# A two-network graph kernel: the second network's first pieces in batches of three slices, some of it on GpSimd, and one column less in two of three multiplications

## The chip, the cores and the metric

One core of a Trainium2 chip runs the whole program. The metric is device time in microseconds (us) of one execution; a kernel's time is the median of its runs. Four engines compute: TensorE (PE in the profile, with its weight loads as PEld), VectorE (DVE), ScalarE (ACT) and GpSimd (POOL). SP issues most transfers, POOL the indirect ones.

## The reference, cut to what matters

Two graph networks run one after the other on the same 100,000 edges and 6,250 nodes of 128 features, each with a residual sum and a layer norm around it:

```python
x = _layernorm(x + _L0_gnn_ref(x, edge_index, edge_type_8, ...), axis=-1)   # relational, three layers
x = _layernorm(x + _L1_gnn_ref(x, edge_index, W_in, b_in, W_out, b_out), axis=-1)
```

The change touches the second network alone:

```python
h = x @ W_in + b_in                                   # 64 columns
deg = jax.ops.segment_sum(ones, row, num_segments=N)
edge_weight = deg_inv_sqrt[row] * deg_inv_sqrt[col]
acc = h
cur = h
for _ in range(3):
    cur = jax.ops.segment_sum(cur[col] * edge_weight[:, None], row, num_segments=N)
    acc = acc + cur
return (acc / 4) @ W_out + b_out
```

So three multiplications by the same sparse matrix A (how often each pair of nodes is joined), with a scaling by `deg_inv_sqrt` before and after each.

## The kernel before, in words

The 6,250 nodes are 49 blocks (`NBLK`) of 128. Nine **slices** (`NSL`) hold every ninth block: slices 0 to 3 have six blocks, slices 4 to 8 five (`FLD` is 6).

**The first network** fills nine tenths of the time: indirect loads on POOL (L1080) bring the rows of `h_d`, PE sums them by one-hot matrices (L1083), DVE adds the sums into `agg` (L1688). Beside it the kernel counts edges into a dense matrix of packed counts in DRAM, `a_d`, two four-bit counts in each byte and four bytes in a 32-bit word.

**The second network** begins when `agg` is whole, in three steps.

1. **Node rows** (L1796 to L1809). In groups of four blocks, PE transposes each block of `agg` into the PSUM tile `pt` (L1801; five buffers, `ps_w`) and multiplies it by `w_mid` into `ph` (L1803; two buffers, `ps_s`). DVE takes mean and variance of each block from `pt` (L1806, L1807, into `mv`). ACT copies `pt` to `x_nm` (L1808) and `ph` to `acc` (L1809). Then, for all 49 blocks at once, `ve` is made (L1810) and `rsqrt` (L769 to L774: one square root on ACT, five small DVE operations) gives `rs`.
2. **First pieces** (L1827 to L1834). For each slice DVE scales `acc` by `rs` (L1830), adds the bias (L1831), scales by `dis` into `z` (L1833), and `split` writes `z` as three bf16 parts that add up to it: ACT copy (L1821), DVE difference (L1822), ACT copy (L1823), DVE difference (L1824). The parts stand in `three[0]`, 192 columns for each block, and a 193rd column (`C3` is 3 * 64 + 1) holds ones.
3. **Three multiplications** (L1881 to L1925, `k` from 0 to 2). For each of nine output slices `sl` and each of nine input slices `c0`: a load of `packed` from `a_d` (L1891), two DVE operations that take out the four-bit counts as 8-bit floats into `u` (L1893, L1894; three buffers), and 30 or 36 matmuls, one for each input block and output block (L1899), into three PSUM tiles `po` out of the same five buffers that `pt` uses. There are 49 * 49 = 2401 matmuls for each `k`. After an output slice, DVE adds the three parts (L1914 to L1916), copies the sum of the ones column (L1918, only for `k == 0`: it is compared with the degrees), scales and adds to `acc`, and splits again for the next `k`. With `k == 1` the first norm of `x_nm` (`first_norm`, L1837 and L1839) is written between the matmuls; with `k == 2` the output head (L1851 to L1877).

**Order.** These parts are written with a tile framework that places all waits and makes each engine's queue itself: instructions are not bound to the order of the source, and a later line can go ahead where the earlier ones have to wait for data or for a buffer. Each engine then runs its queue strictly in order. (Only the first network pins some of its instructions.)

Of the kernel before, what the change touches and what calls it, by code (L numbers as in the profile page):

```python
# [8 lines left out]
F32 = mybir.dt.float32  # L9
# [8 lines left out]
P = 128  # L18
# [501 lines left out]
def sorted_path(  # L520
# [79 lines left out]
    FILL = 16  # L600
    KP = R // 2
# [16 lines left out]
    assert HT % GT == 0 and HC * GPB <= 512 and SUB * R == P and T1 % P1 == 0  # L618
# [1174 lines left out]
    mv = late.tile([P, NBLK, 2], F32, name="mv")  # L1793
    ve = late.tile([P, NBLK], F32, name="ve")
    rs = late.tile([P, NBLK], F32, name="rs")
    for c in range(0, NBLK, 4):  # L1796
        n = min(4, NBLK - c)
        pt = ps_w.tile([P, 512], F32, name="pw")
        ph = ps_s.tile([P, 4, H], F32, name="ps")
        for j in range(n):  # L1800
            nc.tensor.transpose(pt[:, j * P : (j + 1) * P], agg[:, (c + j) * P : (c + j + 1) * P], ident)  # L1801
        for j in range(n):
            nc.tensor.matmul(ph[:, j, :], agg[:, (c + j) * P : (c + j + 1) * P], w_mid, start=True, stop=True)  # L1803
        for j in range(n):
            st = op.tile([P, 6], F32, name="st_r")
            nc.vector.bn_stats(st, pt[:, j * P : (j + 1) * P])  # L1806
            nc.vector.bn_aggr(mv[:, c + j, :], st)  # L1807
        nc.scalar.copy(x_nm[:, c : c + n, :], pt[:, : n * P].rearrange("p (b f) -> p b f", f=P))  # L1808
        nc.scalar.copy(acc[:, c : c + n, :], ph[:, :n, :])  # L1809
    nc.vector.tensor_scalar_add(ve, mv[:, :, 1], EPS)  # L1810
    rsqrt(late, rs, ve, [P, NBLK], "ln1")

    def scale_of(d, sl):
        part = d[:, sl::NSL]
        n = part.shape[1]
        return part[:, :, None].to_broadcast([P, n, H]), n

    def split(to, z, sl):
# [5 lines left out]
        nc.vector.tensor_tensor(t[:, :, 2 * H : 3 * H], z, t[:, :, H : 2 * H], op=OP.subtract)  # L1824


    for sl in range(NSL):  # L1827
        part = acc[:, sl::NSL, :]
        sc_, n = scale_of(rs, sl)
        nc.vector.tensor_tensor(part, part, sc_, op=OP.mult)  # L1830
        nc.vector.tensor_tensor(part, part, b_in_r[:, None, :].to_broadcast([P, n, H]), op=OP.add)  # L1831
        z = tp.tile([P, FLD, H], F32, name="z")
        nc.vector.tensor_tensor(z[:, :n, :], part, scale_of(dis, sl)[0], op=OP.mult)  # L1833
        split(three[0], z[:, :n, :], sl)  # L1834
# [46 lines left out]
    for k in range(3):  # L1881
        cur, nxt = three[k % 2], three[(k + 1) % 2]
        for sl in range(NSL):
            fields = range(0, len(range(sl, NBLK, NSL)))
            po = [ps_w.tile([P, 512], F32, name="pw") for _ in range(FLD // 2)]
            out_of = lambda f: po[f // 2][:, (f % 2) * C3 : (f % 2 + 1) * C3]
            for c0 in range(NSL):
# [9 lines left out]
                for d, b in enumerate(blocks):  # L1897
                    for f in fields:
                        nc.tensor.matmul(out_of(f), bytes_[f % 2][:, d, :, f // 2], cur[:, b, :],  # L1899
# [84 lines left out]
```

## Time and profile before

| | us |
|---|---|
| median of 3 runs (3521.61 to 3531.9) | 3530.43 |
| the profiled execution | 3529.98 |
| its span, first to last instruction | 3528.1 |
| first network and counting, until the last `agg` sum | 0 to 2832.1 |
| node rows (L1801 first) | from 2832.2 |
| first matmul of L1899 | 2867.1 |
| second multiplication begins | 3076.1 |
| third multiplication begins | 3277.1 |
| last matmul of L1899 | 3509.1 |

The profile is one execution. Times in it are microseconds from the start of the span. In a timeline row stand: start, duration, engine, line, operation, written and read tiles, form, count, and in brackets how long the engine had been idle before and what released it. "x2" is two instructions merged into one row. In rows by stretch stand: the stretch, its length, and for each engine the busy time and number of instructions, then PEclk (the clock granted to PE, as a share of the full one), the share of DMA time and GB/s.

### The profile page before, as it was taken

The page shows a single profiled execution, that of the slowest core. Times are in us where ns is not written, and L with a number is a line of the kernel's source. Part 1 is how long each engine was busy: PE and PEld are TensorE (multiplying, and loading weights), DVE is VectorE, ACT ScalarE, POOL GpSimd, SP SyncE. Part 2 cuts the span into 40 slices and gives each one's busy share as a digit, 9 for nine tenths or more (in the row PEclk, how much of TensorE's full clock was granted, in tenths as well). Part 3 has the DMA queues.
Part 4 walks back from the last instruction along what each step waited for, and adds up shares of the span by engine and source line. Part 5 has one row for each costly group of instructions (what it writes and reads, how often), then busy time and mean ns, then how long its engine had stood idle before and what let it go on. Part 6 is the DMA issues. An engine that isn't in the chain of part 4 may idle for free.

```text
span 3528.1 us, 54660 instructions
## 1 busy us (share of the span) xinstructions
PE 2695.5 (76%) x17110; PEld 2161.4 (61%) x17110; DVE 2125.9 (60%) x6259; ACT 916.4 (26%) x2360; POOL 2083.9 (59%) x2083
## 2 busy tenths in 40 slices
PE   5866667776689666677775986666677579999998
PEld 3454447554646555555554565555555479999997
DVE  7766558644644666666475266666643476646566
ACT  3400007521565655555143510000000020000000
POOL 5777777777757777777774767777777700000000
PEclk9955565576588555555855975555567579999999
DMA  6612222232275222222423842222232234545452
GB/s 203 234 54 63 70 56 59 59 94 71 60 249 189 65 69 67 68 72 68 102 72 90 323 127 75 76 76 78 78 94 71 64 103 138 157 133 158 130 141 77
DMA packets 422817, 373.31 MB, mean 106 GB/s; under 512 B 89934, under 2 KB 370286, under 8 KB 422516
## 3 DMA queue, kind: packets, MB, share of 16 engines
q1 hardware_dynamic: 347832, 230.32, 21.3%
q0 software_dynamic: 66240, 135.79, 13.7%
q10 hardware_dynamic: 8444, 3.61, 0.4%
q8 instruction: 136, 2.23, 0.2%
q14 instruction: 165, 1.35, 0.1%
HBM read 250.74 MB, written 178.62 MB: 122 GB/s over the span
## 4 chain that ended last, share of the span: by engine, by line
PE 41%; DMA 37%; DVE 10%; issue 6%; POOL 5%; ACT 0%; DVEq 0%; POOLq 0%; ACTq 0%
DMA gt<-h_d,gidx 36%; PE pw L1899 16%; PE pw L979 7%; PE ps L1083 7%; POOL gt L1080 5%; PE pw L1384 2%; PE pw L1630 2%; DVE row L1616 1%; PE pw L1411 1%; PE pw L992 1%; DVE had L1589 1%; DVE agg L1688 1%; PE ps L1857 1%; PE pw L1558 0%; DVE dst_hot L1612 0%
## 5 line engine op out<-in xcount | busy, mean ns | idle before, releaser
L1080 POOL DMA_INDIRECT gt<-h_d,gidx x1770 | 1768.9, 999 | 546.8 <-DMA gt<-h_d,gidx 235.6
L1083 PE MATMUL ps<-o,gt 128*128 128x48 f32 (+1 forms) x4140 | 1136.3, 389 | 638.1 <-DMA gt<-h_d,gidx 562.1
L1083 PEld LDWEIGHTS ps<-o,gt 128*128 128x128 f32 x4140 | 936.5, 289 | 928.8 <-DMA gt<-h_d,gidx 752.3
L1616 DVE TENSOR_SCALAR row<-iota_c,e_tab,e_tab 128x252 bf16<-128x252 int16 x1232 | 425.7, 352 | 361.0 <-PE pw L1630 357.5
L1899 PE MATMUL pw<-three,u 128*128 128x193 bf16 x7203 | 616.4, 248 | 15.0 <-issue 9.9
L1899 PEld LDWEIGHTS <-u 128*128 128x128 fp8e3 x7203 | 602.9, 98 | 22.6 <-issue 10.0
L1442 ACT ACTIVATE near<-iota_b,e_tab 128x128 bf16<-128x128 bf16 x782 | 304.7, 391 | 747.7 <-PE pd L1455 443.6
L1630 PE MATMUL pw<-dst_hot,row 128*126 128x128 bf16 x2464 | 447.5, 320 | 54.1 <-DVE row L1616 49.5
L1630 PEld LDWEIGHTS <-row 128*126 128x126 bf16 x2464 | 353.9, 224 | 66.8 <-DVE row L1616 57.2
L1589 DVE SCALAR_TENSOR_TENSOR had<-had,keep,pw 126x256 int32<-126x256 int32 x616 | 292.8, 475 | 11.9 <-PE pw L1630 10.9
L979 PE MATMUL pw<-w,xT 128*128 128x512 f32 x588 | 282.2, 613 | 0.0
L1080 POOL DMA_INDIRECT gt<-x_d,xidx x200 | 191.5, 958 | 136.3 <-PE pw L1630 33.2
L1688 DVE TENSOR_TENSOR agg<-agg,ps 128x48 f32 x885 | 179.0, 202 | 142.5 <-PE ps L1083 107.3
L1443 ACT ACTIVATE near<-iota_b,e_tab 128x49 bf16<-128x49 bf16 x782 | 250.5, 321 | 0.0
L1893 DVE TENSOR_SCALAR u<-packed 128x640 int32<-128x640 int32 (+1 forms) x243 | 126.9, 522 | 203.0 <-PE pw L1899 200.6
L1612 DVE TENSOR_TENSOR dst_hot<-iota_f,e_tab 128x512 bf16<-128x512 f32 x308 | 211.6, 687 | 0.1
L980 ACT COPY hs<-pw 128x512 f32<-128x512 f32 x294 | 171.2, 586 | 121.4 <-PE pw L979 115.5
L1358 ACT CAST x<-xc 128x512 bf16<-128x512 f32 x21 | 13.0, 621 | 673.5 <-PE pw L1384 541.5
L1446 ACT ACTIVATE near<-near,ones 128x708 bf16<-128x708 bf16 x196 | 172.9, 882 | 5.7
L1384 PE MATMUL pw<-x,u 128*128 128x385 bf16 x735 | 172.0, 375 | 0.0
L1111 DVE TENSOR_TENSOR z<-z,ps 128x56 f32 x300 | 63.3, 211 | 179.5 <-PE ps L1083 164.2
L979 PEld LDWEIGHTS pw<-w,xT 128*128 128x128 f32 x588 | 105.2, 194 | 89.7 <-issue 84.1
(400 smaller groups left out, 2174.2 us busy)
## 6 DMA issues: line engine op xcount, KB each, us to landing
a_d<-had SPq DMA_DIRECT2D x616, 126.0 KB
h_d<-hs SPq DMA_DIRECT2D x147, 512.0 KB
packed<-a_d SPq DMA_DIRECT2D x135, 320.0 KB
packed<-a_d SPq DMA_DIRECT2D x108, 384.0 KB
gt<-h_d,gidx POOLq DMA_INDIRECT x1770
c_d<-had SPq DMA_DIRECT2D x62, 196.0 KB
packed<-c_d SPq DMA_DIRECT2D x21, 448.0 KB
x_d<-xc SPq DMA_DIRECT2D x24, 256.0 KB
```

What stands on the lines that cost most here:

```text
L979: nc.tensor.matmul(ph, xT[:, b * P : (b + 1) * P], w[:, c : c + 512], start=True, stop=True)
L1080: nc.gpsimd.indirect_dma_start(out=gt, out_offset=None, in_=table[:, :], in_offset=bass.IndirectOffsetOnAxis(ap=at[:, t : t + 1], axis=0))
L1083: pin(nc.tensor.matmul(pa, gt, o, start=first_, stop=last))
L1384: nc.tensor.matmul(sums[d][:, :C3D], us[d % 2][:, i, :, d // 2], x3[:, i, :], start=(c == 0 and i == 0), stop=(c * CH + i == NBLK - 1))
L1442: nc.scalar.activation(near[:, j, :P], iota_b, AF.Abs, bias=src_lo[:, k : k + 1], scale=-1.0)
L1443: nc.scalar.activation(near[:, j, P:], iota_b[:, :NBLK], AF.Abs, bias=src_blk[:, k : k + 1], scale=-1.0)
L1589: pin(nc.vector.scalar_tensor_tensor(now[:HB, : 2 * P], had[:HB, : 2 * P], keep[:HB, s : s + 1], p[:HB, : 2 * P], op0=OP.mult, op1=OP.add))
L1612: pin(nc.vector.tensor_tensor(hots[i // TS], iota_f[:, None, :].to_broadcast([P, TS, P]), flat(e_lo)[:, i : i + TS, None].to_broadcast([P, ...
L1616: pin(nc.vector.tensor_scalar(rows[i][:, : 2 * HB], iota_c[:, : 2 * HB], e_col[:, s, j : j + 1], e_val[:, s, j : j + 1], op0=OP.is_equal, ...
L1630: pin(nc.tensor.matmul(sums[s][:HB, c * P : (c + 1) * P], row[:, c * HB : (c + 1) * HB], hots[u // TS][:, u % TS, :], start=(j == 0 and c ...
L1688: pin(nc.vector.tensor_add(to, to, pa))
L1899: nc.tensor.matmul(out_of(f), bytes_[f % 2][:, d, :, f // 2], cur[:, b, :], start=(b == 0 and f % 2 == 0), stop=(c0 == NSL - 1 and d == m ...
```

## The change: what it does

- Node rows are made by slices, not by consecutive blocks: `node_rows` takes three blocks (or the two that are left of five) of a slice, so there are 18 groups in place of 13. The work on each block is the same. ACT copies `acc` before `x_nm`.
- They come in three batches of three slices (`SLB`): the blocks of slices 0 to 2 (18 blocks), `ve` and `rsqrt` for these alone, their first pieces; then slices 3 to 5 (16 blocks), then 6 to 8 (15 blocks). `mv`, `ve` and `rs` get 54 columns, so that a batch is a regular part of them; a POOL memset fills the five that no block has.
- In the second and third batch two of the five DVE operations of the first pieces go to POOL: the bias (L1831) and the last difference (L1824), 12 instructions.
- L1899 reads and writes 193 columns for `k == 0` alone, 192 for `k` of 1 and 2.

```diff
+    SLB = 3
...
-    for c in range(0, NBLK, 4):
-        n = min(4, NBLK - c)
+    mv = late.tile([P, FLD * NSL, 2], F32, name="mv")
+    nc.gpsimd.memset(mv[:, NBLK:, :], 1.0)
...
+    def node_rows(blocks):
+
+        n, at = len(blocks), slice(blocks[0], blocks[-1] + 1, NSL)
         pt = ps_w.tile([P, 512], F32, name="pw")
         ph = ps_s.tile([P, 4, H], F32, name="ps")
...
+        nc.scalar.copy(acc[:, at, :], ph[:, :n, :])
+        nc.scalar.copy(x_nm[:, at, :], pt[:, : n * P].rearrange("p (b f) -> p b f", f=P))
...
-    def split(to, z, sl):
+    def split(to, z, sl, third=nc.vector):
...
-        nc.vector.tensor_tensor(t[:, :, 2 * H : 3 * H], z, t[:, :, H : 2 * H], op=OP.subtract)
-    for sl in range(NSL):
+        third.tensor_tensor(t[:, :, 2 * H : 3 * H], z, t[:, :, H : 2 * H], op=OP.subtract)
+    def first_parts(sl, third):
...
         nc.vector.tensor_tensor(part, part, sc_, op=OP.mult)
-        nc.vector.tensor_tensor(part, part, b_in_r[:, None, :].to_broadcast([P, n, H]), op=OP.add)
+        third.tensor_tensor(part, part, b_in_r[:, None, :].to_broadcast([P, n, H]), op=OP.add)
...
+        split(three[0], z[:, :n, :], sl, third)
+
+    for s0 in range(0, NSL, SLB):
+        for sl in range(s0, s0 + SLB):
+            blocks = list(range(sl, NBLK, NSL))
+            for i in range(0, len(blocks), FLD // 2):
+                node_rows(blocks[i : i + FLD // 2])
+        var = by_slices(mv[:, :, 1], s0)
+        nc.vector.tensor_scalar_add(by_slices(ve, s0), var, EPS)
+        rsqrt(late, by_slices(rs, s0), by_slices(ve, s0), [P, FLD, SLB], f"ln1_{s0}")
+        for sl in range(s0, s0 + SLB):
+            first_parts(sl, nc.gpsimd if s0 else nc.vector)
...
-            out_of = lambda f: po[f // 2][:, (f % 2) * C3 : (f % 2 + 1) * C3]
+            cols = C3 if k == 0 else C3 - 1
+            out_of = lambda f: po[f // 2][:, (f % 2) * C3 : (f % 2) * C3 + cols]
...
-                        nc.tensor.matmul(out_of(f), bytes_[f % 2][:, d, :, f // 2], cur[:, b, :],
+                        nc.tensor.matmul(out_of(f), bytes_[f % 2][:, d, :, f // 2], cur[:, b, :cols],
```

## The prediction

> **What bounds the kernel now.** I read the chain of waits on the page first: over the whole span it is the gathers of the first network, which the change leaves alone.
>
> ```profile
> DMA gt<-h_d,gidx 36%; PE pw L1899 16%; PE pw L979 7%; PE ps L1083 7%; POOL gt L1080 5%; PE pw L1384 2%; PE pw L1630 2%; DVE row L1616 1%; PE pw L1411 1%; PE pw L992 1%; DVE had L1589 1%; DVE agg L1688 1%; PE ps L1857 1%; PE pw L1558 0%; DVE dst_hot L1612 0%
> ```
>
> So what counts is L1899's 16% and the short stretch before it. Second, the busy times by stretch from the last sum of `agg` (2832.1) on; the last row is a steady slice of the second multiplication.
>
> ```profile
> 2832.20:2850.50 18.30, 18.27 (x90) 18.30 (x91) 8.12 (x55) 5.02 (x12) 0.00 (x0) 0.50 0.64 191
> 2850.50:2857.20 6.70, 6.54 (x61) 6.24 (x60) 6.17 (x43) 3.64 (x11) 0.00 (x0) 1.00 0.00 0
> 2857.20:2867.10 9.90, 0.00 (x0) 0.03 (x1) 9.35 (x27) 4.07 (x10) 0.00 (x0) 0.68 0.42 119
> 2867.10:2878.10 11.00, 11.00 (x108) 10.52 (x108) 11.00 (x27) 4.55 (x10) 0.00 (x0) 0.83 0.01 3
> 2878.10:2881.00 2.90, 0.04 (x2) 0.01 (x1) 2.90 (x8) 1.37 (x4) 0.00 (x0) 1.00 0.00 0
> ...
> 3100.90:3125.40 24.50, 24.50 (x296) 24.50 (x294) 12.75 (x33) 1.04 (x2) 0.00 (x0) 1.00 0.47 132
> ```
>
> The columns are PE, PEld, DVE, ACT, POOL, then PE's clock. PE bounds the first 18.3 us at half clock (DVE is busy 8.12 of them), PE and DVE together the next 6.7. Then DVE alone bounds 9.9 us in which PE has nothing, and again 2.9 us. A steady slice has PE full and DVE half empty. Third, the chain and the timeline give the paces:
>
> ```profile
> 2838.22 1.60 PE ps L1803 x8
> 2840.68 1.60 PE ps L1803 x8
> ...
> 3079.86 226.13 PE pw L1899 x2703
> ```
> ```profile
> 2861.75 1.03 DVE L1830 TENSOR_TENSOR acc<-acc,rs 128x384 f32<-128x384 f32 x2
> 2862.70 1.02 DVE L1831 TENSOR_TENSOR acc<-acc,b_in_r 128x384 f32<-128x384 f32 x2
> ...
> 2867.10 11.03 PE L1899 MATMUL pw<-three,u 128*128 128x193 bf16 x108 [9.94 <-issue]
> ...
> 2880.37 0.57 DVE L1893 TENSOR_SCALAR u<-packed 128x768 int32<-128x768 int32 x1
> ```
>
> Groups of four blocks start 2.46 us apart at half clock: 0.614 us a block. L1899 takes 226.13 / 2703 = 83.66 ns a matmul at full clock, 24.6 us for a six-block slice. A six-block DVE operation of the first pieces takes (2862.70 - 2861.75) / 2 = 0.47 us, a five-block one 0.405 (the same two rows at 2875: 0.81 for two). L1899 starts when slice 0's parts are written (2867.0). After 108 matmuls, which are the first three input slices, PE stands still because the fourth `u` (2880.37) stood in DVE's queue behind the first pieces of later slices.
>
> Slice 0 of the first multiplication took 2867.1 to 2898.3, 31.2 us against 24.6 steady: 2.9 of standing still and 3.7 of half clock (3.8 us at its start, 3.4 after the stop, at half rate). Slice 1 lost 1.6 waiting for DVE to empty PSUM.
>
> **The change, part by part.** *Node rows.* 49 blocks as before; 18 groups cost PE nothing extra, since the pace is the sum over blocks. PE finishes 18 blocks at 2832.2 + 18 x 0.614 = 2843.3, about when DVE has their statistics (0.26 us a block, L1806 start to start); so DVE is idle 6 us instead of some 10. That is where the batches gain.
>
> *DVE's work before the first matmul.* The queues are not in source order (L1837, written for `k == 1`, runs from 2883.7 to 2922.5, in the first multiplication), but earlier lines go first where they are ready: no `u` was made until the statistics were at their end (2857.2), though PE could have used none sooner. The matmuls also need three of the five PSUM buffers that the transposes of all 49 blocks are waiting for. So I expect L1899 behind nearly all node rows, and its first `u` behind nearly all statistics. From 2843.3: `rsqrt` 1.2 (six operations of about 0.2 around 2860), first pieces of three slices 15 x 0.47 = 7.05, 31 more blocks of statistics 31 x 0.263 = 8.15, second `rsqrt` 1.2, the two opening DVE operations of slices 3 to 5, 6 x 0.43 = 2.6, the third `rsqrt` 1.2, the first `u` 0.93 (two operations, 0.47 each): 22.3, so 2865.6. Between 2864.4 (third `rsqrt` later) and this plus what POOL costs.
>
> *POOL's share.* It takes 12 DVE operations away, about 5 us of DVE, but the bias addition stands between two DVE operations of its slice, and behind L1833 waiting in DVE's queue stand the statistics and `u`, which PE waits for. No POOL arithmetic on two tensors is in the trace. Its nearest rows:
>
> ```profile
> L1155 POOL IOTA iota_s<- 128x616 f32 x1 | 0.7, 668 | 0.0
> L1782 POOL MEMSET three<- 128x49 bf16 x2 | 0.5, 384 | 3.1 <-PE ps L1083 3.1
> ...
> masks.py:199 POOL TENSOR_SCALAR_AFFINE_SELECT ident<-ident 128x128 f32<-128x128 f32 x1 | 0.3, 282 | 0.0
> ```
>
> With 0.10 us fixed (the one-element memset), the iota's rate gives 0.46 us for 384 elements, the selection, which reads one tensor, 0.65, the strided memset 2.3. I take 0.9: above the selection, since two tensors are read. Six of the twelve fall before the first matmul. Whether DVE can run beside them no row shows; between nothing and 6 x 0.9 = 5.4 I take half, 2.7: start at 2868.3, **1.2 later** than 2867.1. The ends are 2864.4 (2.7 earlier) and, at 2.3 with DVE held throughout, 2865.6 + 13.8 = 2879.4 (12.3 later).
>
> The Trainium skill speaks against this part: "SBUF — State Buffer", section "Who interferes with whom", says that a DVE operation with two SBUF inputs and a GpSimd operation that reads SBUF exclude each other for a whole instruction. "GPSIMD Engine Reference", section 3.1, gives some 2.6 cycles an element at 1.2 GHz for two inputs, an estimate of 0.83 us for 384. By these the start would be 2865.6 + 6 x 0.83 = 2870.6 and the time 3526.4.
>
> *Slice 0.* At the start only slices 6 to 8 are left to DVE: 9 operations (3.7 us) and eight `u` (7 us), plus POOL's, against 24.6 us of matmuls. So the 2.9 stop goes, and the second stretch of half clock with it; the first stays, as PE is half idle before. 31.2 becomes 24.6 + 1.9 = 26.5: **4.7 less**, between 1.8 (the stop stays) and 6.6. What hides the `u` is DVE's spare half; if that is gone, the stop of 2.9 is the price.
>
> *Slice 1.* Its stop comes from first norms queued before the emptying of PSUM, and these remain, only earlier. Between 0 and 1.6 I take **0.8 less**. The third `rsqrt`, five more ACT copies a side and the memset run beside DVE's queue and PE: nothing; uncovered, under 2 us.
>
> *The column.* 4802 matmuls lose one. The rate by columns: at full clock twelve matmuls of 385 columns start within 1.97 us,
>
> ```profile
> 2639.95 0.99 PE L1384 MATMUL pw<-x,u 128*128 128x385 bf16 x5
> ...
> 2641.92 0.98 PE L1384 MATMUL pw<-x,u 128*128 128x385 bf16 x5
> ```
>
> 164 ns each, so (164 - 83.66) / 192 = 0.418 ns a column: **2.0 less**. Beyond its columns (193 x 0.418 = 80.7) a matmul costs 3.0 ns; both forms have an odd count, and an even one may save part of that. The 128-column matmuls of L1630 start 55 ns apart at their closest, 1.5 beyond theirs; so at most 0.42 + 1.5 ns, 9.2 in all. I take 2.0, by the row of the same form, with the odd count.
>
> The Trainium skill ("TensorE: Matmul & The Clock Gate", section "Wait — 56ns, not 53.3ns?") has N / 2.4 GHz plus about 2.5 ns, an estimate of 82.5 ns for 192 columns; against the row's 83.66 that would save 5.6 us, and the time would be 3520.5.
>
> The sum: + 1.2 - 4.7 - 0.8 - 2.0 = - 6.3. The profiled span of 3528.1 becomes 3521.8. The execution around it took 3529.98, 0.45 below the median of 3530.43, so on the median: **3524.1**.
>
> **The rivals.** *Early start.* The first matmuls slip into PE's queue as soon as slice 0's parts exist: 2843.3 + 1.2 + 5.3 (slice 0's row from L1830 to L1824) + 0.9 = 2850.7. For it: lines do go ahead (L1933, behind the whole first multiplication, ran at 2856.97). Against: it did so only at the last group, and the PSUM buffers. Then DVE sets the end of slice 0: 2843.3 + three `rsqrt` 3.6 + 7.05 + 8.15 + 18 operations 7.5 + nine `u` 7.8 + half of twelve POOL operations 5.4 + the last 30 matmuls 2.5 = 2885.3, 13.0 before 2898.3. With 0.8 and 2.0: 3514.6; 3509 if POOL holds nothing up.
>
> *POOL holds DVE.* One mechanism: the bias additions of slices 3 to 5 at 2.3 us, DVE standing behind each, first matmul at 2879.4. + 12.3 - 4.7 - 0.8 - 2.0 = + 4.8: 3535.2, slower than before. Without POOL's delay the first matmul is 1.5 earlier than before, and the other terms give 7.5; so it decides from (1.5 + 7.5) / 6 = 1.5 us of held DVE per operation. For it: DVE was without a pause from 2856 to 2924, so anything that holds it is seen. Against: the selection's 0.28.
>
> *The column does nothing*, because the weight load (98 ns mean) and not the columns sets the pace: 3526.1. Against: L1384 has the same load and a pace that grew by its columns alone.
>
> **How the numbers follow.** What a measurement of this kernel can tell from no change is about 0.3%, 10.6 us. Forecast 0.52 (its own range 3514 to 3531: up by POOL's full 0.9 for six, 2.7, half the stop and slice 1's 0.8; down by the earlier start, 3.9, and most of the column's rest), early start 0.25, POOL holds DVE 0.15, column nothing 0.08. Faster by over 0.3% (below 3519.8): 0.13 of the forecast (full clock, even count), 0.20 of the early start, 0.02 of the last: 0.35. Slower (above 3541): 0.06 of the third, if it also holds slices 6 to 8, and 0.02 from the others: 0.08. Within: 0.57. The range, 3508 to 3536, leaves out about 0.08 at each end.
>
> **What would show it.** First matmul of L1899 between 2864 and 2871 (2851: early start; 2875 or later: POOL). In its first slice no idle time over 1 us on PE, and 26 to 27 us long. POOL's operations near 0.9 us, and DVE's rows of the second batch with idle time before L1833 released by POOL, under 3 us in all. 83.2 ns a matmul for `k == 1`, against 82.5 if the even count helps. The prediction is wrong if the time before 2832 moves by more than the runs differ, or if the first matmul's wait is for something other than DVE.

## The result and the profile after

The changed kernel takes 3540.35 us (median of 7 runs, 3534.83 to 3543.62) where the kernel before took 3526.45 beside it (median of 7, 3519.11 to 3531.9): a ratio of 1.0038, with a 95% interval of 1.0026 to 1.0051. The forecast was 3524.1, with a range of 3508 to 3536. The change makes the kernel slower by 9 to 18 us, so the prediction was wrong, in sign and in range.

The chain of waits of the changed kernel is much as before (the first network's gathers 31% against 36%, the multiplications 16% in both); the stretch that counts can't be read from it:

```profile
DMA gt<-h_d,gidx 31%; PE pw L1916 16%; PE ps L1084 9%; PE pw L980 7%; POOL gt L1081 4%; PE pw L1385 3%; PE pw L1631 3%; DVE row L1617 1%; PE pw L1412 1%; PE pw L993 1%; DVE had L1590 1%; DVE agg L1689 1%; PE ps L1873 1%; PE pd L1385 1%; PE pw L1559 0%
```

I measure with what I call the **stretch**: from the first transpose of the node rows to the first matmul of the second multiplication (`k == 1`). It holds all of the change but the column. It was 243.8 us before (2832.2 to 3076.1, rounded) and is 252.6 in the changed kernel's profile (2830.2 to 3082.8). Its busy times by part, in the columns of the prediction (PE, PEld, DVE, ACT, POOL, PEclk, DMA share, GB/s):

```profile
2830.20:2848.20 18.00, 17.98 (x90) 18.00 (x91) 7.24 (x50) 5.49 (x18) 0.00 (x0) 0.50 0.79 198
2848.20:2853.70 5.50, 5.46 (x49) 5.16 (x47) 3.91 (x13) 2.95 (x11) 0.00 (x0) 1.00 0.00 0
2853.70:2858.40 4.70, 0.00 (x0) 0.00 (x0) 3.94 (x12) 3.03 (x7) 0.00 (x0) 0.64 0.01 2
2858.40:2872.07 13.67, 3.61 (x13) 1.92 (x14) 13.62 (x65) 7.03 (x17) 5.70 (x6) 0.50 0.00 1
2872.07:2900.36 28.29, 27.26 (x295) 25.57 (x295) 27.53 (x89) 2.75 (x7) 6.32 (x6) 0.94 0.39 111
2900.36:2931.24 30.88, 26.55 (x297) 25.92 (x296) 24.02 (x83) 1.03 (x2) 0.00 (x0) 0.94 0.43 123
3107.50:3131.97 24.47, 24.47 (x297) 24.47 (x295) 12.81 (x33) 1.03 (x2) 0.00 (x0) 1.00 0.47 133
```

Four rows lead up to the first matmul, which comes at 2872.07, 41.8 us after the first transpose; before it was 34.9. The fifth and sixth rows are output slices 0 and 1 of the first multiplication: 28.3 us (31.2 before) and 30.9 (26.2 before). The last is a steady slice at 192 columns: 24.47 against 24.58. So the first matmul is 7.0 us later, slice 0 gives 2.9 back, slice 1 loses 4.7: 8.8 in all, and the column gives 1.8.

The first four rows hold the main point. DVE is busy 7.24 + 3.91 + 3.94 + 13.62 = 28.7 of 41.8 us, idle 13.1. Before, by the prediction's rows, it was busy 8.12 + 6.17 + 9.35 = 23.6 of 34.9, idle 11.2. The batches put 5.1 us more work ahead of the first matmul and did not fill DVE's idle time with it: 5.1 + 1.9 is the 7.0. Rows by line say what the idle time waited for (line, form, count, then busy time and mean ns, then idle time before it and its releaser), first before, then in the changed kernel:

```profile
L1806 DVE BATCH_NORM_STATS2 st_r<-pw 128x6 f32<-128x128 f32 x49 | 13.3, 276 | 10.8 <-PE pw L1801 10.5
```
```profile
L1810 DVE BATCH_NORM_STATS2 st_r<-pw 128x6 f32<-128x128 f32 x49 | 12.9, 273 | 6.6 <-PE pw L1805 6.6
...
L1827 DVE TENSOR_TENSOR z<-z,three 128x384 f32<-128x384 f32 (+1 forms) x6 | 2.9, 528 | 2.4 <-ACT three L1826 2.3
...
L771 DVE RECIPROCAL ln_a<-ln_a 128x18 f32<-128x18 f32 x2 | 0.5, 266 | 4.3 <-ACT ln_a L770 4.3
```

The waiting for PE's transposes did go down, from 10.8 to 6.6. But 6.6 of waiting for ACT came in its place (4.3 for the root, 2.3 for a cast), where it had been 0.5.

DVE's timeline says where it stood (start, duration, engine, line, operation, tiles, form, count; in brackets the idle time before, and its releaser):

```profile
2842.49 0.16 DVE L1847 TENSOR_SCALAR ve<-mv 128x18 f32<-128x18 f32 x1
...
2842.72 0.27 DVE L1810 BATCH_NORM_STATS2 st_r<-pw 128x6 f32<-128x128 f32 x1
2847.29 0.27 DVE L771 RECIPROCAL ln_a<-ln_a 128x18 f32<-128x18 f32 x1 [4.30 <-ACT ln_a L770]
...
2854.41 1.03 DVE L1827 TENSOR_TENSOR z<-z,three 128x384 f32<-128x384 f32 x2 [2.31 <-ACT three L1826]
...
2863.31 2.14 DVE L1835 TENSOR_TENSOR acc<-acc,rs 128x384 f32<-128x384 f32 x3
2865.37 2.68 DVE L1838 TENSOR_TENSOR z<-acc,dis 128x384 f32<-128x384 f32 x3
2867.97 1.35 DVE L1827 TENSOR_TENSOR z<-z,three 128x384 f32<-128x384 f32 x3
```

The first batch's `ve` was there at 2842.6 (forecast: 2843.3), but the reciprocal that needs its square root started 4.7 us later, and the first difference stood 2.31 us for its cast. Both releasers are ACT. ACT's timeline beside it:

```profile
2846.82 0.32 ACT L1812 COPY acc<-ps 128x192 f32<-128x192 f32 x1 [1.11 <-PE ps L1807]
2847.03 0.22 ACT L770 ACTIVATE ln_a<-ve 128x18 f32<-128x18 f32 x1
...
2853.10 0.71 ACT L1812 COPY acc<-ps 128x192 f32<-128x192 f32 x2 [0.40 <-PE ps L1807]
2853.86 0.93 ACT L1826 CAST three<-z 128x384 bf16<-128x384 f32 x2
```

ACT was not busy; it was idle 1.11 us before the copy at 2846.82, waiting for PE. The square root stood behind that copy of the second batch in ACT's queue, and the casts behind copies of the third. PE made the rows ahead of the root at half clock, and so the root was paced by PE.

PE's and then POOL's timeline:

```profile
2853.47 0.19 PE L1950 MATMUL ps<-all_first,ones 128*1 128x1 f32 x2
2858.42 0.69 PE L1805 MATMUL pw<-ident,agg 128*128 128x128 f32 x2 [4.75 <-ACT x_nm L1813]
...
2872.07 10.94 PE L1916 MATMUL pw<-three,u 128*128 128x193 bf16 x109 [8.92 <-DVE mv L1811]
...
2906.29 5.87 PE L1916 MATMUL pw<-three,u 128*128 128x193 bf16 x49 [4.12 <-DVE sums L1935]
```
```profile
2864.00 3.30 POOL L1836 TENSOR_TENSOR acc<-acc,b_in_r 128x384 f32<-128x384 f32 x3 [35.30 <-DVE acc L1835]
2869.15 2.40 POOL L1829 TENSOR_TENSOR three<-z,three 128x384 bf16<-128x384 f32 x3 [1.85 <-ACT three L1828]
```

PE stood 4.75 us with transposes still to do, until ACT had copied an earlier `x_nm` out of PSUM, and the clock fell back to 0.50 (the fourth row by part); it stood 8.92 until the first `u`, which came behind the last statistics; and 4.12 between slices 0 and 1 until DVE had emptied PSUM. POOL's operations took 1.1 and 0.8 us each (1.1 and 1.0 in the third batch).

The stop of 4.12 goes back to the same lateness. These are the first operations that empty PSUM after slice 0, in DVE's timelines before and in the changed kernel:

```profile
2899.89 0.50 DVE L1914 COPY z<-pw 128x128 f32<-128x128 f32 x2
```
```profile
2905.10 0.47 DVE L1931 COPY z<-pw 128x128 f32<-128x128 f32 x2
```

That is 67.7 and 74.9 us after the first transpose: DVE is 7.2 us later, hardly more than the 7.0 at the first matmul. What PE gained in slice 0 it stood out again at the end of it.

### The profile page after: what moved, and what is told of

It reads as the page before. It is cut to its first block, busy times and chain, and to the rows that moved or that the text cites. A ratio compares the mean times of both kernels' runs of the same rounds, so it can differ in the third digit from the quotient of the medians.

```text
span 3533.0 us, 54703 instructions
## 1 busy us (share of the span) xinstructions
PE 2696.3 (76%) x17110; PEld 2157.8 (61%) x17110; DVE 2126.1 (60%) x6259; ACT 918.4 (26%) x2372; POOL 2095.2 (59%) x2096
## 4 chain that ended last, share of the span: by engine, by line
PE 44%; DMA 32%; DVE 10%; issue 9%; POOL 4%; ACT 0%; DVEq 0%; POOLq 0%; SPq 0%; ACTq 0%
DMA gt<-h_d,gidx 31%; PE pw L1916 16%; PE ps L1084 9%; PE pw L980 7%; POOL gt L1081 4%; PE pw L1385 3%; PE pw L1631 3%; DVE row L1617 1%; PE pw L1412 1%; PE pw L993 1%; DVE had L1590 1%; DVE agg L1689 1%; PE ps L1873 1%; PE pd L1385 1%; PE pw L1559 0%
## 5 line engine op out<-in xcount | busy, mean ns | idle before, releaser
L1916 PE MATMUL pw<-three,u 128*128 128x192 bf16 (+1 forms) x7203 | 615.1, 247 | 15.1 <-DVE mv L1811 8.9
L1081 POOL DMA_INDIRECT gt<-x_d,xidx x200 | 193.1, 965 | 135.3 <-PE pw L1631 33.7
```

The source lines that it names most:

```text
L1081: nc.gpsimd.indirect_dma_start(out=gt, out_offset=None, in_=table[:, :], in_offset=bass.IndirectOffsetOnAxis(ap=at[:, t : t + 1], axis=0))
```

## The experiments

Three theories came out of this profile. Theory 1: POOL's share holds DVE and costs more than it saves. Theory 2: the waits come from ACT's queue, where the root and the casts stand behind copies paced by PE. Theory 3: slice 1's stop comes from first norms that stand ahead of the emptying of PSUM in DVE's queue. A fourth question is why the medians differ by 13.9 us where the two profiles' stretches, less the column, differ by 6.9.

The table has what the profiles of all kernels show of the stretch; "rise" is the time from the first transpose until the granted clock goes from 0.5 to 1.0, "first" the time until the first matmul of the first multiplication, then slices 0 and 1 and the stretch, all in us. The ratio is to the kernel before, run beside it on the same chip. All of a row but its ratio is from one profiled execution.

| kernel | rise | first | slice 0 | slice 1 | stretch | ratio, 95% interval |
|---|---|---|---|---|---|---|
| before | 18.2 | 34.9 | 31.2 | 26.2 | 243.8 | |
| before_again | 8.5 | 30.2 | 29.7 | 26.4 | 237.9 | 1.0009 (0.9986 to 1.0031) |
| before_third | 3.5 | 27.9 | 30.8 | 26.2 | 236.4 | 0.9985 (0.9965 to 1.0005) |
| cols_only | 13.2 | 32.5 | 31.3 | 26.2 | 241.6 | 0.9997 (0.9987 to 1.0006) |
| changed kernel | 18.0 | 41.8 | 28.3 | 30.9 | 252.6 | 1.0038 (1.0026 to 1.0051) |
| after_again | 18.2 | 41.9 | 28.3 | 30.9 | 252.8 | 1.0053 (1.0040 to 1.0066) |
| after_third | 17.9 | 41.8 | 28.3 | 30.9 | 252.6 | 1.0039 (1.0017 to 1.0060) |
| pool_only | 18.1 | 34.8 | 33.9 | 29.1 | 249.4 | 1.0026 (1.0015 to 1.0036) |
| batch_dve | 18.3 | 42.6 | 26.0 | 29.2 | 249.4 | 1.0038 (1.0025 to 1.0051) |
| batch_dve_act | 18.1 | 39.9 | 27.2 | 26.5 | 245.2 | 1.0011 (0.9988 to 1.0034) |
| batch_dve_late | 15.5 | 38.7 | 26.6 | 24.6 | 241.5 | 0.9995 (0.9972 to 1.0018) |
| norms_late | 10.6 | 31.2 | 30.9 | 24.6 | 238.3 | 1.0023 (0.9998 to 1.0048) |
| in_turn | 18.1 | 33.1 | 27.2 | 24.6 | 236.5 | 0.9974 (0.9954 to 0.9994) |
| in_turn_again | 17.6 | 32.9 | 27.1 | 24.6 | 236.2 | 0.9986 (0.9958 to 1.0014) |
| in_turn_third | 39.3 | 34.4 | 27.0 | 24.6 | 237.6 | 0.9992 (0.9971 to 1.0013) |
| in_turn_fourth | 16.0 | 32.1 | 26.7 | 24.6 | 235.0 | 0.9992 (0.9967 to 1.0018) |
| no_batch_in_turn | 15.7 | 33.7 | 27.4 | 24.6 | 237.3 | 0.9990 (0.9965 to 1.0016) |
| no_batch_again | 18.1 | 34.8 | 26.4 | 24.6 | 237.4 | 0.9974 (0.9949 to 0.9999) |

The first comparison and after_again, cols_only, batch_dve and pool_only ran on chips where the kernel before takes 3520 to 3526 us. All the others ran on chips where it takes 3987 to 3997: there the first network, which no experiment alters, is some 470 us longer, and runs scatter by 15 us or more either way. The stretch is not slower there, so I compare stretches across chips, and times only with the kernel before beside them.

**The changed kernel again (after_again).**

> The changed kernel again, unaltered, to see what of its profile belongs to it and what to one execution. In its profile the stretch from the first transpose of the node rows to the first matmul of the second multiplication (k == 1) took 252.6 us against 243.8 before; that explains about 7 of the 13.9 us between the medians. If the waits come from the order of the queues (theory), it is 252 to 254 again, the first matmul of the first multiplication 41 to 43 us after that transpose (34.9 before), and the median 3535 to 3545. Rival A: the rest lies in the first network, whose queues hold the same instructions in the same order: the first transpose starts at 2836 or later (2832.2 before, 2830.2 in the changed kernel's first profile). Rival B: the stretch itself varies from one execution to the next, up to 260.

Stretch 252.8, first matmul at 41.9, median 3538.83: the waits belong to this kernel and not to one execution, to within 0.2 us. That they come from the order of the queues is what the next experiments test. Rival A (a later first network) is not seen, with the first transpose at 2832.7, and rival B is not seen in any of this kernel's three profiles.

**The column alone (cols_only).** The matmuls of `k` 1 and 2 take 192 columns:

```diff
-            out_of = lambda f: po[f // 2][:, (f % 2) * C3 : (f % 2 + 1) * C3]
+            cols = C3 if k == 0 else C3 - 1
+            out_of = lambda f: po[f // 2][:, (f % 2) * C3 : (f % 2) * C3 + cols]
...
-                        nc.tensor.matmul(out_of(f), bytes_[f % 2][:, d, :, f // 2], cur[:, b, :],
+                        nc.tensor.matmul(out_of(f), bytes_[f % 2][:, d, :, f // 2], cur[:, b, :cols],
```

> The kernel before with nothing of the change but the column: the second and third multiplications take 192 columns. If the column is worth 0.418 ns a matmul (as in the prediction) the second and third together are 2.0 us shorter, a six-block slice 24.46 instead of 24.58; by the changed kernel's steady slices (24.47) it is 0.374 ns and 1.8 us. If the even count were worth 1.5 ns more: 24.0 a slice and 9 us. Rival, the column does nothing: 24.58. Nothing moves before the first matmul of k == 1. Time 3524 to 3526 where the kernel before has 3526.

A six-block slice took 24.47, and the second and third multiplications together (431.1 us against 433.0) lost 1.9. The even count brings nothing more. In the median (3517.75 against 3520.1) this can't be told from no change.

**The batches without POOL (batch_dve).**

```diff
-            first_parts(sl, nc.gpsimd if s0 else nc.vector)
+            first_parts(sl, nc.vector)
```

> The changed kernel with GpSimd's twelve operations back on DVE. Theory 1 (GpSimd's share costs more than it saves): before the first matmul DVE gets six operations more, 6 x 0.43 = 2.6 us, and is rid of the stretch of nine operations beside GpSimd by 0.57 us each (5.1) and of waiting for it: first matmul 39 to 40 us after the first transpose instead of 41.9, and the stretch to k == 1 about 249 to 251. Theory 2 (the waits come from the order of the ACT and DVE queues, not from GpSimd): the 4.3 and 2.3 us of idle DVE for the root and the casts and the 4.1 us stop of slice 1 remain, the first matmul is 42 to 44.5 us after the first transpose, and the stretch to k == 1 is 252 to 256. In both it stays above the 243.8 of the kernel before.

First matmul at 42.6 and both idle times still there, as theory 2 has it:

```profile
2842.95 0.27 DVE L771 RECIPROCAL ln_a<-ln_a 128x18 f32<-128x18 f32 x1 [4.30 <-ACT ln_a L770]
...
2850.24 1.03 DVE L1827 TENSOR_TENSOR z<-z,three 128x384 f32<-128x384 f32 x2 [2.48 <-ACT three L1826]
```

This is DVE's timeline of batch_dve. But slices 0 and 1 got shorter by 2.3 and 1.7, which theory 1 has and theory 2 hasn't, and the stretch is 249.4. Both have a part: the batches alone cost 5.6 us of stretch, POOL's share 3.2 on top of them.

**POOL's share without batches (pool_only).** The order of the kernel before; its bias addition and third difference go to POOL for slices 3 to 8:

```diff
+        third = nc.gpsimd if sl > 2 else nc.vector
...
-        nc.vector.tensor_tensor(part, part, b_in_r[:, None, :].to_broadcast([P, n, H]), op=OP.add)
+        third.tensor_tensor(part, part, b_in_r[:, None, :].to_broadcast([P, n, H]), op=OP.add)
```

> The kernel before, with GpSimd doing the bias addition and the third difference of slices 3 to 8 as in the changed kernel, without batches and with 193 columns. Theory 1 (DVE is held beside GpSimd): GpSimd takes 12 operations, 5.0 us, from DVE, and about fifteen DVE operations beside it take 0.57 us more each, 8.6: the stretch from the first transpose to k == 1 goes from 243.8 to 246 or 248. Rival, GpSimd's work is free: the stop of 2.9 us in slice 0 goes, and the stretch is 239 to 242. The first matmul stays at 35 us after the first transpose in both, since slices 0 to 2 are DVE's.

The stretch is 249.4 at the same rise at which the kernel before had 243.8, and the median is 8 us over it. POOL's share does harm by itself. The cause stands in PE's and then DVE's timeline of pool_only:

```profile
2874.53 0.34 PE L1900 MATMUL pw<-three,u 128*128 128x193 bf16 x1 [4.16 <-DVE u L1894]
2875.66 19.07 PE L1900 MATMUL pw<-three,u 128*128 128x193 bf16 x200 [0.79 <-DVE u L1895]
2897.57 27.67 PE L1900 MATMUL pw<-three,u 128*128 128x193 bf16 x311 [2.83 <-DVE sums L1919]
```
```profile
2873.36 1.11 DVE L1894 TENSOR_SCALAR u<-packed 128x768 int32<-128x768 int32 x1
2874.40 1.21 DVE L1895 TENSOR_SCALAR u<-packed 128x768 int32<-128x768 int32 x1
...
2876.51 0.48 DVE L1894 TENSOR_SCALAR u<-packed 128x640 int32<-128x640 int32 x1
```

The fourth `u`, for which PE stands, takes 1.11 + 1.21 us while POOL works, against 0.57 for each in the kernel before. PE's stop in slice 0 grows from 2.9 to 4.16 + 0.79, slice 1's from 1.4 to 2.83. The clock is at half for 6.8 us after the first of these, where it was 3.4 before, and for another 3.4 after the second, where it had not fallen.

**The order of ACT's queue (batch_dve_act).** A dependence without a semaphore, which only orders the queue, holds the copies of a later batch behind an earlier batch's root and casts:

```diff
+    def behind(ins, last):
+        if last is not None:
+            tc.add_manual_dep(ins.ins, last.ins.name,
+                              mybir.DependencyInfo(mybir.DependencyClass.NoSync, mybir.DependencyReason.DATA),
+                              reason="order of queue")
...
-        nc.scalar.copy(acc[:, at, :], ph[:, :n, :])
+        behind(nc.scalar.copy(acc[:, at, :], ph[:, :n, :]), gates[0])
```

`gates[0]` is the first batch's root while the second batch's rows are made, and its last cast for the third's.

> The batches all on DVE, as in batch_dve, with one thing changed: on ACT the copies of the second batch's node rows stand behind the first batch's square root, and those of the third behind the first batch's last cast; DVE's queue is the same. Theory 2 (the waits come from ACT's queue): DVE's idle 4.3 us before the reciprocal and 2.5 before the first difference of batch_dve shrink to under 1.5 together, and the first matmul comes 36 to 38 us after the first transpose instead of 42.6; the stretch to k == 1 is 243 to 245 instead of 249.4. Rival: DVE had nothing else to do then (the node rows come from PE at half clock), so the same idle time appears before the statistics instead: first matmul at 41 to 43, stretch 248 to 250. Slice 1 keeps its stop (29.2 us) in both.

In DVE's timeline the first batch's root no longer has an idle time ahead of it, and 1.58 (for a cast) and 1.05 (for the second batch's root) are left:

```profile
3334.16 1.03 DVE L1836 TENSOR_TENSOR z<-z,three 128x384 f32<-128x384 f32 x2 [1.58 <-ACT three L1835]
...
3342.69 0.27 DVE L771 RECIPROCAL ln_a<-ln_a 128x18 f32<-128x18 f32 x1 [1.05 <-ACT ln_a L770]
```

The first matmul came only 2.7 us sooner (39.9, expected 36 to 38), since part of the rival holds too: DVE's idle time ahead of statistics grew from 6.6 to 7.8, and PE still stood 3.34 us in the node rows. The stretch of 245.2 is 4.2 shorter: 2.7 in the start, 2.7 in slice 1, and 1.2 lost in slice 0. I had expected nothing of slice 1, but the traces settle it. DVE's queue has the same operations in the same order in both kernels and no idle time from the first matmul to the emptying of PSUM, so it gets there 2.6 us sooner, about what it gained at the start. PE's stop is 1.71 us instead of 2.78, and after the shorter one the clock stayed at 1.0, where batch_dve lost 3.4 us to half clock: 1.1 + 1.7 = 2.7, within rounding.

**The first norms held back as well (batch_dve_late), and alone on the kernel before (norms_late, with the column).**

```diff
-    def first_norm(b):
-        nc.vector.tensor_scalar(x_nm[:, b, :], x_nm[:, b, :], mv[:, b, 0:1], rs[:, b : b + 1],
-                                op0=OP.subtract, op1=OP.mult)
+    def first_norm(b, last):
+        norm = nc.vector.tensor_scalar(x_nm[:, b, :], x_nm[:, b, :], mv[:, b, 0:1], rs[:, b : b + 1],
+                                       op0=OP.subtract, op1=OP.mult)
+        behind(norm, last)
```

`last` is the `u` operation of the norm's own step in `k == 1`.

> As batch_dve_act, and the first norms, which are written for k == 1 but ran in the first two slices of k == 0, are held behind the u of their own step in k == 1. Theory 3 (slice 1's stop comes from first norms ahead of the emptying of PSUM in DVE's queue): slice 1 is 24.6 us instead of 29.2, the slices of k == 1 stay at 24.47 and 20.38, since DVE is half empty there, and the stretch to k == 1 is 4.6 us shorter than in batch_dve_act: 238.5 to 240.5. Rival: the stop has another cause (the third batch's pieces or the u), slice 1 stays above 27; or the norms cost the same later, and a slice of k == 1 grows by over 0.5.

> The kernel before with the first norms held in k == 1 and 192 columns for k of 1 and 2, no more. Theory 3: slice 1 is 24.6 us instead of 26.2 to 26.4, slice 0 keeps its stop (29.5 to 31.3), k == 1 and 2 together are 1.8 shorter; the stretch is 1.6 to 1.8 shorter than in the kernel before at the same rise of the clock, and the time 3 to 4 us less, which a median can hardly tell from nothing. Rival: the stop of slice 1 has another cause, and it stays over 26.

Slice 1 is 24.6 in both, and the slices of `k == 1` stay at 24.47 and 20.38: theory 3 holds, and the norms cost nothing where DVE is half empty. Slice 0 of norms_late is 30.9, as long as before. The stretch of batch_dve_late (241.5) was a little above its range, and a part of its gain is an earlier rise (15.5 us), so it is slice 1 that counts here. In the time of norms_late (1.0023) the gain does not show, nor could 3 us do so where the interval is 20 us wide.

**All of it in turn (in_turn, in_turn_again, in_turn_third, in_turn_fourth).** All on DVE: a first batch of slices 0 to 2, a second of the other six, whose pieces are written one slice at a time behind a `u` of the first multiplication; ACT's queue and the norms as above; 192 columns.

```diff
-    for s0 in range(0, NSL, SLB):
+    for s0, size in ((0, SLB), (SLB, NSL - SLB)):
...
+                if k == 0 and sl == 0 and c0 + SLB < NSL:
+                    first_parts(c0 + SLB, nc.vector)
```

> What the theories together suggest, all on DVE: a first batch of slices 0 to 2 made during the node rows (ACT's queue in the order of batch_dve_act), the other six slices in a second batch whose pieces are written slice by slice after the u of the first multiplication that they follow, the first norms held in k == 1, 192 columns for k of 1 and 2. If the order of the queues is what costs the changed kernel its time, the first matmul comes 28 to 32 us after the first transpose (34.9 and 32.4 in the two profiles of the kernel before's queues), slice 0 takes 26 to 29 us, slice 1 24.6, the stretch to k == 1 is 230 to 236, and the time 8 to 13 us under the kernel before. Rival: DVE's sum up to the first u sets the start whatever the order, and what is taken from before the first matmul comes back in slice 0: stretch 240 or more, time within 4 us of the kernel before.

> in_turn again, for a second profile and for its time on another chip, if one is given. Expected as measured: first matmul 33 us after the first transpose, slice 0 27.2, slice 1 24.6, stretch 236.5 plus or minus 1, since in all batched kernels the clock rose 15.5 to 18.3 us after the first transpose; time 5 to 12 us under the kernel before. Rival: by the first profile's luck with the clock; a stretch of 240 or more.

> in_turn a third time, beside the two above on one chip: stretch 236 to 237 as twice before, 16 us under the changed kernel's and 2 to 7 under that of the kernel before, and 1.8 for the column: ratio to the kernel before 0.9975 to 0.999, and the median 14 to 20 us under the changed kernel's. Rival: the medians don't follow the stretch, and it is not faster than the kernel before on a chip where the interval is narrow.

> in_turn once more, for its time: stretch 236 to 238 as three times before. On a chip where the kernel before takes 3520 to 3530 us and its runs lie within some 10 us, the ratio to it is 0.9965 to 0.999 if medians follow the stretch (4 to 7 us less there, and 1.8 for the column); on a chip of 3990 us the interval will take in 1 again or just miss it. Rival: the median is not below that of the kernel before.

The stretch was 236.5, 236.2, 237.6 and 235.0: some 16 us under the changed kernel's. On in_turn_third's chip the changed kernel had a median of 4010.65 and in_turn 3989.83. PE's timeline of in_turn shows what is left:

```profile
3338.75 0.44 PE L1814 MATMUL pw<-ident,agg 128*128 128x128 f32 x2 [3.34 <-ACT x_nm L1822]
...
3347.32 30.89 PE L1932 MATMUL pw<-three,u 128*128 128x193 bf16 x336 [1.10 <-DVE mv L1820]
```

From the first matmul on PE runs without a stop into slice 1. The first matmul is later than I had expected (33.1, not 28 to 32) and the stretch half a microsecond above its range, since PE still stands 3.34 us in the node rows, loses the clock, and makes the rest of them at half rate. Against the kernel before, the four ratios give together 0.9985 (weighted by their intervals: 0.9974 to 0.9997): probably faster, by some 6 us of 3990. Only one of the four intervals leaves out 1, and none of them is from a chip of the faster kind.

**The order without batches (no_batch_in_turn, no_batch_again).** The kernel before's node rows and single root; slice 0's pieces first, slice k + 1's behind the `u` of input slice k; norms and column as above.

> The kernel before's node rows and single root, no batch and nothing on GpSimd; only the order is changed: before the first matmul the pieces of slice 0 alone, those of slice k + 1 written after the u of input slice k in the first output slice, first norms held in k == 1, 192 columns for k of 1 and 2. If order is what counts and batches add nothing: first matmul about 3 us earlier than in the kernel before (slice 0's pieces alone take some 4 us instead of 5.3 interleaved with two others), 28 to 32 us after the first transpose depending on when the clock rises, no stop in slice 0 (26 to 28 instead of 31.2 and 29.7), slice 1 24.6, the stretch to k == 1 is 231 to 236 (before 237.9, 241.5 and 243.8), and the time 6 to 12 us under the kernel before. Rival: the batches are needed to fill DVE's idle time during the node rows: stretch not below in_turn's 236.5, time less than 5 us under the kernel before.

> no_batch_in_turn once more. Its first profile had the rise of the clock 15.8 us after the first transpose and a stretch of 237.3; if the stretch follows the rise as in the kernel before, it is 231 to 234 for a rise at 4 to 10 us and 237 to 239 for one at 16 to 18. Rival: it is 237 whatever the rise.

Stretch 237.3 and 237.4, ratios 0.9990 and 0.9974 (the second with an interval that just leaves out 1). The stop in slice 0 is gone (27.4 and 26.4) and slice 1 is 24.6, so most of in_turn's gain needs no batch. By the marks set beforehand (stretch not below 236.5, less than 5 us of time) the first run is nevertheless the rival's, if by a microsecond. The first matmul was not 3 us earlier: 34.8 at a rise of 18.1 is the kernel before's 34.9. The trace says why: up to the first matmul DVE ran the very operations of the kernel before, in the same order, with the pieces of further slices still between those of slice 0, and PE stood 9.94 us as before. The new order in the source took hold only behind the first matmul, so what slice 0's pieces alone would give at the start is untested. Whether an early rise shortens this kernel's stretch stays open, as neither execution had one.

**The spread of the stretch (before_again, before_third, after_third).** The two kernels unaltered, for further profiles.

> The kernel before, unaltered, for a second profile of it. Its stretch from the first transpose of the node rows to the first matmul of k == 1 was 243.8 us, and 241.5 in the kernel with only the column, which has the same queues up to there. If the medians differ by more than the stretches because the kernel before ran shorter elsewhere (first network), the first transpose comes at 2822 to 2828 in a run near the median, with the stretch 241 to 244 again. Rival: the stretch itself varies, and is 238 or less. Time equal to the kernel before: 3520 on the chip of the first four runs, 3526 on the one of the first comparison.

> The kernel before, for a third profile. The stretch from the first transpose to k == 1 goes with the moment at which the granted clock rises in it: 8.5 us after the first transpose 237.9, 13.3 us 241.5, 18.3 us 243.8. Theory 5 (part of the gap between the medians is that the queues before meet an earlier rise, and finish the node rows at full clock, more often than the batched ones): rise at 8 to 14 us, stretch 238 to 242. Rival: rise at 17 us or more and 243 to 244, as in the batched kernels, and the rest of the gap lies in the first network: first transpose 5 us or more earlier than in after_third on the same chip, beside its medians.

> The changed kernel, for a third profile: the clock rises 18 us after the first transpose, as in the two so far, drops again when PE waits for slice 0's casts and ACT's copies, and the stretch is 252.5 plus or minus 1; ratio to the kernel before 1.003 to 1.006 on a chip of 3520 us. Rival: with an earlier rise the stretch shrinks as that of the kernel before does, to 250 or less.

The changed kernel's stretch was 252.6 a third time, with the rise at 17.9. That of the kernel before was 237.9 and 236.4, with rises at 8.5 and 3.5: the first is the rival's value (the stretch itself varies), the second lies below the range expected. Busy times by part of before_third and before_again, cut at the rise and at the last node row:

```profile
3296.51:3300.11 3.60, 3.60 (x18) 3.60 (x19) 1.12 (x8) 0.86 (x2) 0.00 (x0) 0.51 1.12 332
3300.11:3313.84 13.73, 13.73 (x130) 13.73 (x130) 12.53 (x87) 7.16 (x18) 0.00 (x0) 1.00 0.53 157
3313.84:3324.36 10.52, 0.47 (x5) 0.19 (x5) 9.96 (x31) 4.70 (x12) 0.00 (x0) 0.66 0.39 112
```
```profile
3300.63:3309.11 8.48, 8.48 (x42) 8.48 (x43) 3.44 (x23) 2.08 (x5) 0.00 (x0) 0.50 1.06 317
3309.11:3320.30 11.19, 11.19 (x106) 11.19 (x106) 10.18 (x71) 5.91 (x15) 0.00 (x0) 1.00 0.01 2
3320.30:3330.90 10.60, 0.53 (x6) 0.27 (x6) 10.04 (x31) 4.72 (x12) 0.00 (x0) 0.62 0.39 111
```

PE is busy throughout the node rows either way, and after them DVE has the same 10.5 us to the first matmul; what differs is how long PE works at half rate. With the single root the node rows run through, so an early rise is kept. This is theory 5 of the expectations, and it accounts for a part: in the four profiles with the kernel before's queues up to there (before, before_again, before_third, cols_only) the stretch is 239.9 on average, and the changed kernel's 252.7 less the column's 1.8 is 11 us over it. The medians differ by 13.9, 18.7 (after_again) and, from the ratio, 15.6 us (after_third), with intervals of 9 to 18, 14 to 23 and 7 to 24. The first and the third are covered. On the chip of after_again at least 3 us are left by this average, which no profile shows. The first network varies too: on the two faster chips the first transpose came at 2824.6 to 2832.7. Nor is it shown that the batches make the rise late: of the eight executions with the node rows of the kernel before, four had it at 15.7 us or later too.

## Why the prediction was wrong, point by point

Against the profile before, the stretch was to be 4.3 us shorter (+ 1.2 - 4.7 - 0.8) and was 8.8 longer. Of these 13.1 us the first matmul has 5.8, slice 1 5.5 and slice 0 1.8.

- **"DVE is idle 6 us instead of some 10. That is where the batches gain."** This is the step that failed. The idle time ahead of statistics did go from 10.8 to 6.6; but the 22.3 us that follow were a sum of DVE's work with no wait for ACT in it, as if DVE could go from one piece to the next. Between 2842.57 and the first matmul at 2872.07 lie 29.5 us, of which DVE stood 4.30 + 2.31 for ACT: 22.9 of work, near enough to the sum. The root stood in the sum as one of six operations of 0.2 us, the casts not at all, and of what else ACT had to do I had written "run beside DVE's queue and PE: nothing; uncovered, under 2 us". It was 6.6. Root and casts stood in ACT's queue behind copies that PE paced. batch_dve_act, which changes that queue alone, took most of the waiting away, and showed too that some of it comes back ahead of the statistics: the gain is 2.7 us in the start and 4.2 in the stretch. DVE was still idle 10.4 us there, not 6.
- **First matmul 1.2 later.** It was 7.0 later (batch_dve: 7.7). The idle time of DVE ahead of it was not 4 us less but 1.9 more. The place of the first `u`, behind nearly all statistics, was as forecast.
- **POOL.** 0.9 us an operation was measured as 0.8 to 1.1, and the held-up time before the first matmul, for which I took 2.7 and, in the estimate from the skill's pages, 6 x 0.83 = 5.0, was about 2.1: nine DVE operations from 2863.31 on took 5.9 us instead of 3.8 (three at 0.47 and six at 0.40, by the rows of batch_dve). What failed is the place: I counted it only up to the first matmul. In slices 0 and 1 it costs 2.3 and 1.7 more: in slice 0 it is `u` that is held up, with PE behind it, and although POOL's last operation ends at 2884.0, DVE then comes later to the emptying of PSUM as well. It also hardly shows as I said it would, as idle time released by POOL (0.76 us in all, in the third batch): it shows as DVE operations of up to twice the length. And DVE was not without a pause from 2856 to 2924 before, as I had read: it stood 1.20 us before 2885.93.
- **Slice 0, 4.7 less.** The size was right without POOL: 5.1 less in batch_dve. With POOL it was 2.9.
- **Slice 1, 0.8 less.** It was 4.7 more. I had seen that the first norms stand ahead of the emptying of PSUM and took them to be "only earlier". But DVE was as late at the emptying (7.2 us) as at the first matmul (7.0), while PE had caught up 2.9 in slice 0. The stop grew from 1.42 to 4.12 us, and brought 3.4 us of half clock with it. batch_dve_late shows the norms to be the cause of what was left of it: held back, 24.6.
- **The column, 2.0 less.** 1.8 to 1.9: right, and so was leaving the odd count at nothing. 24.47 us for 294 matmuls are 83.2 ns, not 82.5.
- **The rivals.** "POOL holds DVE" has the right direction and the right engine but not the right mechanism: not 2.3 us an operation with DVE standing behind the bias additions, but DVE's own operations stretched. As a cause by itself it would have been worth a rival: pool_only is 8 us slower. No rival had ACT's queue: putting it in order gives 4.2 us of stretch, taking POOL's share away 3.2. The early start did not happen (the first `u` came behind the last statistics), and "the column does nothing" is excluded by the 1.9 us of cols_only.

The sizes, by stretch at a rise of about 18: batches alone + 5.6, POOL's share alone + 5.6, the two together + 8.8, less 1.8 for the column. Without POOL, with ACT's queue in order and the norms held, the batched kernel comes from 252.6 to 241.5 (at a rise of 15.5). The profile that the prediction started from was itself the longest of the four with these queues (243.8, on average 239.9), which no single profile could show.

## What to carry to other kernels

A step that is cut into batches to fill one engine's idle time sends its small helpers (a root, a cast) through the queue of another engine; look there for what stands ahead of them and at whose pace it moves, since an idle engine can be a late one. Work moved to a second engine is only free if its partner's operations keep their length, and if what they make late is not what the bound engine waits for. What made the stretch shorter here was order: pieces written just behind the operation that the next matmul waits for, and late work held where the engine is half empty. An order in the source is not yet one in the queue, as no_batch_in_turn shows; the trace has to say that it took hold.

## What the runs showed of the hardware

- **The clock's rise is not a fixed time of busy work.** PE was busy without a gap from the first transpose on, and the clock rose after 3.5, 8.5, 13.2 and 18.2 us, with the same instructions up to there; with it the stretch of the kernel before went from 236.4 to 243.8. The Trainium skill ("TensorE: Matmul & The Clock Gate", section "What's actually happening") gives about 3.4 us of sustained work for it. One of these executions agrees; in the others PE was fully busy for 2.5 to 5.4 times as long, and the measurement decides. In the ten executions of batched kernels the rise came at 15.5 us or later; why stays open.
- **A stop of PE cost the clock for longer than the stop.** In the changed kernel the clock rose at 18.0, fell 1.4 us into PE's stop of 4.75 us (at 2855.0) and came back after 20.5 us, 3.4 into the first multiplication; PE had little to do for most of that. in_turn is the plainer case: after the stop of 3.34 us the clock was at half for 13.7 us, in 12.1 of which PE was busy. Between slices 0 and 1, stops of 1.42 us (the kernel before) and 1.71 (batch_dve_act) left the clock at 1.0, and stops of 2.78 (batch_dve), 2.83 (pool_only) and 4.12 (the changed kernel) each brought 3.4 us of half clock.
- **DVE beside POOL.** `u`, which reads one tensor, took 1.11 to 1.21 us instead of 0.57 while POOL ran an operation on two tensors. That agrees with the Trainium skill ("SBUF — State Buffer", section "Who interferes with whom"), which counts this kind of DVE operation among those that can take the port pair shared with GpSimd; in the prediction I had applied the rule only to operations with two inputs.
- **The same kernel took 13% longer on four of the chips.** There the first network took 3282 to 3314 us up to the first transpose, on the others 2825 to 2833, with the same instructions. In the profile of before_again the matmul of L1630 has 707.6 us of idle time before it, 54.1 in that of the kernel before; what is behind this stays open.
